# First sweep of a cross-attention: keys projected in quarters and queries in pieces, one a round, each with a PSUM bank of its own

## The chip, the cores and the metric

The kernel runs on one core of one Trainium2 chip. The metric is the device time of one execution in microseconds (us); the figure for the kernel before is the median of three runs.

## The reference

The reference is one block of a Perceiver: a cross-attention of 2 x 512 latent tokens to a context of 2 x 8192 tokens, a windowed self-attention, and a mixture of 16 experts with a shared feed-forward part. The change touches the first part alone:

```python
q = layernorm(x) @ Wq.T + bq          # 2 x 512 tokens, 512 features = 16 heads of 32
k = ctx @ Wk.T + bk                   # 2 x 8192 tokens
v = ctx @ Wv.T + bv
att = einsum('bhqd,bhkd->bhqk', q, k) / sqrt(32)
att = where(mask == 0, -inf, att)
out = einsum('bhqk,bhkd->bhqd', softmax(att, axis=-1), v)
x = x + (out @ Wo.T + bo)
```

All of it is in float32, with the mask and the maxima in bfloat16 inside the kernel where it subtracts them.

## The kernel before, in words

**Units, chunks, slots.** A unit is one batch entry `b` and one group `g` of four heads (128 features): 8 units. The 8192 context tokens of a unit are 16 chunks (`NKC`) of 512 tokens (`KC`). A slot is one chunk of one unit; there are 128 (`NS`). The softmax needs the maximum over all 8192 keys before the first exponential, so the kernel sweeps a unit twice: in slot `n` it projects the keys of chunk `n`, in slot `n + 1` it takes that chunk's maxima (`max_part`), and in slot `n + 18` (`LAG` is 18) it computes the scores again, their exponentials and their products with the values. Three units are thus worked on at a time in most of the kernel. In the first 18 slots, numbered 0 to 17, there is nothing to exponentiate yet: only keys, maxima, the queries, and from slot 16 on the values. The change is about these slots and what comes ahead of them.

**Rounds.** A slot is a loop of four rounds, `i` = 0 to 3 (the `for i in range(4)` of the slot loop). `max_part(slot - 1, i)` handles the query tokens `128 i` to `128 i + 127`. For the first 17 chunks it takes its early form: two double-bank PSUM tiles from the pool `pairs` (3 tiles, 6 banks), each for two heads; four float32 products of 32 x 128 queries by 32 x 512 keys (L276), one for each head, then four one-row bfloat16 products that add the mask row (L282); then VectorE reduces each double tile to its maxima (`tensor_reduce`, L287, 128 x 1024 in, 128 x 2 out, into the SBUF tile `mst`). With three tiles and two used a round, the first tile of a round is free at once, and the second is the one that VectorE reduced first in the round before.

**What else a round holds.** Rounds 0 and 1 of a slot project the two halves of its keys, `project_k(slot, half)`: 16 products with 32-column weights and 256 tokens (L239), four side by side in the four column groups of the array, into one PSUM bank, and one ScalarE instruction that adds the bias and writes SBUF (L243). From slot 16 on, rounds 2 and 3 project the values (L255, then VectorE at L260). Round 3 of slots 1 to 12 takes one entry of the list `later`: three queries of batch 0 (`query(0, g)`), the statistics of batch 1 (`query_norm(1)`), its four transposes (`query_in`, L98), its four queries. A query is four products with 128-column weights and 512 tokens (L173) and a ScalarE instruction (L177). One matmul in the code is two instructions in the trace where its operands are float32.

**PSUM.** During the first 18 slots the pool `ps` has two banks that serve everything but the maxima: transposes, queries, keys, values, and the two small tiles of `max_finish`. At slot 18 these pools close and one of 8 banks opens.

**Order of the work.** Each engine runs its own instructions in order; a scheduler places them nearly as the code writes them. Loads go out on SyncE's queue in the order written, each waiting for its buffer: tokens of batch 0, `wq`, `wk`, context chunk 0, tokens of batch 1, `wv`, then a context chunk (1 MB, 4 buffers) and a mask row for each slot. The mask row of chunk 0 must wait until `mask_rows` has turned the mask and written it to DRAM from ScalarE's queue (L192, L196). Ahead of slot 0 the code normalizes and transposes the four token blocks of batch 0, projects query (0, 0), then calls `mask_rows` and `load_mask(0)`; slot 0 itself projects the keys of chunk 0.

Of the kernel before, what the change touches and what calls it, by code (L numbers as in the profile page):

```python
# [10 lines left out]
F32 = mybir.dt.float32  # L11
# [3 lines left out]
AF = mybir.ActivationFunctionType  # L15
ALU = mybir.AluOpType
AX = mybir.AxisListType
PSUM = bass.MemoryType.PSUM

P = 128  # L20
B, S, D = 2, 512, 512
T = B * S
S2 = 8192
H, DK = 16, 32
G = 4
DC = D // P
# [8 lines left out]
KC = 512  # L35
NKC = S2 // KC
# [7 lines left out]
def perceiver_kernel(  # L44
# [8 lines left out]
    nc = tc.nc  # L53
# [8 lines left out]
    def load_x(b):  # L62
        nc.sync.dma_start(
            out=x_sb[:, ts(b, NT // B), :],
            in_=x[ts(b, S), :].rearrange("(n p) d -> p n d", p=P),
        )
# [22 lines left out]
    def normalized(dst, n, mv, rs):  # L89
        nc.vector.tensor_scalar(  # L90
            dst, x_sb[:, n, :], mv[:, n, 0:1], rs[:, n : n + 1], ALU.subtract, ALU.mult
        )

    def transposed(dst, src, ps):

        tp = ps.tile([P, 4, P], F32, tag="ps", name="tp")
        for c in range(4):
            nc.tensor.transpose(tp[:, c, :], src[:, ts(c, P)], ident)  # L98
        nc.scalar.copy(dst, tp)
# [17 lines left out]
    with ExitStack() as es:  # L117
# [5 lines left out]
        pp = es.enter_context(tc.tile_pool(name="a_p", bufs=4))  # L123
        dram = es.enter_context(tc.tile_pool(name="a_dram", bufs=1, space=bass.MemoryType.DRAM))

        first_ps = ExitStack()
        ps = first_ps.enter_context(tc.tile_pool(name="a_ps1", bufs=2, space=PSUM))
        pairs = first_ps.enter_context(tc.tile_pool(name="a_pairs", bufs=3, space=PSUM))

        def load_w(src, pool, tag):  # L130
            t = pool.tile([P, DC, D], F32, tag=tag, name=tag)
            nc.sync.dma_start(out=t, in_=src.rearrange("(c p) f -> p c f", p=P))
            return t

        bq_c = cp.tile([P, G], F32, name="bq_c")
# [15 lines left out]
        nc.vector.memset(mrep, 0.0)  # L151
        junk = cp.tile([P, KC], BF16, name="junk")

        wq_sb = load_w(wq, pp, "p")
        wk_sb = load_w(wk, cp, "wk_sb")


        qT = cp.tile([P, G, T], F32, name="qT")
        xnT, ln = {}, {}

        def query_norm(b):
            ln[b] = layernorm_stats(tmp, range(b * (NT // B), (b + 1) * (NT // B)))
            xnT[b] = pp.tile([P, DC, S], F32, tag="p", name="xnT")

        def query_in(b, c):
            xn = tmp.tile([P, D], F32, tag="row", name="xn")
            normalized(xn, b * (NT // B) + c, *ln[b])
            transposed(xnT[b][:, :, ts(c, P)], xn, ps)

        def query(b, g):  # L170
            pq = ps.tile([P, S], F32, tag="ps", name="pq")
            for c in range(DC):
                nc.tensor.matmul(  # L173
                    pq, lhsT=wq_sb[:, c, ts(g, P)], rhs=xnT[b][:, c, :],
                    start=(c == 0), stop=(c == DC - 1),
                )
            nc.scalar.activation(qT[:, g, ts(b, S)], pq, AF.Identity, bias=bq_c[:, g : g + 1])  # L177

        mbias = cp.tile([P, B, S2 // P], F32, name="mbias")
        mrow = dram.tile([B, S2 // P, P], F32, name="mrow")  # L180
# [2 lines left out]
        def mask_rows():  # L183


            nc.vector.tensor_scalar(mbias, mask_i, 0.0, -BIG, ALU.is_equal, ALU.mult)
            for b in range(B):
                tp = ps.tile([P, P], F32, tag="ps", name="tpk")
                nc.tensor.transpose(tp[0 : S2 // P, :], mbias[:, b, :], ident)
                mt = tmp.tile([S2 // P, P], F32, name="mt")  # L190
                nc.scalar.copy(mt, tp[0 : S2 // P, :])
                nc.scalar.dma_start(out=mrow[b], in_=mt)  # L192
                if b == 0:
                    mh = tmp.tile([S2 // P, P], BF16, name="mh")
                    nc.scalar.mul(mh, tp[0 : S2 // P, :], -1.0)
                    nc.scalar.dma_start(out=mrow_h, in_=mh)  # L196
# [3 lines left out]
        NS = len(chunks)  # L200
# [3 lines left out]
        def load(slot):  # L204

            for b, j in {(units[u][0], j) for u, j in wanted(slot)}:
                t = ctxp.tile([P, DC, KC], F32, tag="ctx", name="ctx_t")
                nc.sync.dma_start(
                    out=t, in_=ctxT[b, :, ts(j, KC)].rearrange("(c p) s -> p c s", p=P)
                )  # L210
                ctx_t[slot, b] = t

        def load_mask(slot):

            u, j = chunks[slot]
            early = slot + 1 < LAG
            t = mp.tile(
                [P, KC], BF16 if early else F32, tag="mkh" if early else "mk", name="mk", bufs=3
            )
            rows = mrow_h if early else mrow[units[u][0]]  # L220
            nc.sync.dma_start(
                out=t,
                in_=rows[ts(j, KC // P), :].rearrange("c p -> (c p)").partition_broadcast(P),
            )
            mk_t[slot] = t

        def wanted(slot):
            return [chunks[s] for s in (slot, slot - NKC) if 0 <= s < NS]

        def project_k(slot, half):  # L230
            u, j = chunks[slot]
            b, g = units[u]
            if half == 0:
                k_t[slot] = kp.tile([P, KC], F32, tag="k", name="kt")
            hs = ts(half, KC // 2)
            pk = ps.tile([P, KC // 2], F32, tag="ps", name="pk")
            for c in range(DC):
                for h in range(4):
                    nc.tensor.matmul(  # L239
                        pk[ts(h, DK), :], lhsT=wk_sb[:, c, ds(g * P + h * DK, DK)],  # L240
                        rhs=ctx_t[slot, b][:, c, hs], start=(c == 0), stop=(c == DC - 1),
                    )
            nc.scalar.activation(k_t[slot][:, hs], pk, AF.Identity, bias=bk_c[:, g : g + 1])  # L243
# [138 lines left out]


        load(0)
        load_x(1)
        wv_sb = load_w(wv, cp, "wv_sb")
        query_norm(0)
        for c in range(NT // B):
            query_in(0, c)
        query(0, 0)  # L390
        mask_rows()
        load_mask(0)
        later = [lambda g=g: query(0, g) for g in range(1, G)]
        later += [lambda: query_norm(1)]
        later += [lambda c=c: query_in(1, c) for c in range(NT // B)]
        later += [lambda g=g: query(1, g) for g in range(G)]

        waiting = None
        for slot in range(NS + LAG):
            if slot == LAG:  # L400
                first_ps.close()
                ps = es.enter_context(tc.tile_pool(name="a_ps", bufs=8, space=PSUM))
            if slot + 1 < NS + NKC:
                load(slot + 1)
            elif slot + 1 == NS + NKC:
                wo_sb = load_w(wo, ctxp, "ctx")
                wqkv_t = [load_w(wqkv[:, ts(i, D)], ctxp, "ctx") for i in range(3)]
            if slot + 1 < NS:
                load_mask(slot + 1)
            s = slot - LAG  # L410
            for i in range(4):
                if 1 <= slot <= NS:
                    max_part(slot - 1, i)
                if s >= 0:
                    scores(s, i)
                if waiting is not None:
                    values(*waiting)
                waiting = (s, i) if s >= 0 else None
                if s >= NKC and chunks[s][1] == 1:
                    finish(chunks[s][0] - 1, i)  # L420
                if i < 2 and slot < NS:
                    project_k(slot, i)
                if i == 3 and slot > 0 and later:
                    later.pop(0)()
                if i >= 2 and NKC <= slot < NS + NKC:
                    project_v(slot, i - 2)
            if 1 <= slot <= NS and chunks[slot - 1][1] == NKC - 1:
                max_finish(chunks[slot - 1][0])
# [23 lines left out]
    ps = ctx.enter_context(tc.tile_pool(name="c_ps", bufs=8, space=PSUM))  # L452
# [21 lines left out]
    xnT, aT, hT = {}, {}, {}  # L474


    with ExitStack() as es:
# [249 lines left out]
        for k in range(len(items) + 3):  # L727
            i, n = divmod(k, NBQ)
# [74 lines left out]
    for b in range(B):  # L803
        sT = sTp.tile([P, SH // P, S], F32, tag="sT", name="sT")
        for f in range(SH // P):
            pair = []
            for wts in (shg, shu):
                pf = ps.tile([P, S], F32, tag="ps", name="pf")
                for c in range(DC):
                    nc.tensor.matmul(  # L810
                        pf, lhsT=wts[f // 4][:, c, ts(f % 4, P)], rhs=hT[b][:, c, :],
                        start=(c == 0), stop=(c == DC - 1),
# [17 lines left out]
        for j in range(4):  # L830
            po = ps.tile([P, D], F32, tag="ps", name="pso")
            for f in range(SH // P):
                nc.tensor.matmul(  # L833
                    po, lhsT=sT[:, f, ts(j, P)], rhs=shd[f // 4][:, f % 4, :],
                    start=(f == 0), stop=(f == SH // P - 1),
# [120 lines left out]
```

## Time and profile before

| what | value |
|---|---|
| median of 3 runs | 3814.18 us (3814.16 to 3819.29) |
| profiled execution | 3813.35 us |
| its span, first to last instruction | 3811.6 us |
| PE busy in the span | 3741.4 us, 98% |
| VectorE (DVE) busy | 2293.9 us, 60% |
| ScalarE (ACT) busy | 1601.8 us, 42% |
| GpSimd (POOL) busy | 2069.0 us, 54% |
| first reduction of a maximum (L287) | at 28.28 us |
| first product of slot 18 (L295) | at 254.19 us |

The span is 1.75 us shorter than the time of its execution. In the profile PE is the matmul unit and PEld its weight loads. A row of the timeline gives start, duration, engine, line, operation, the program's names as out<-in, shapes and count, and in brackets how long the engine was idle before it and what ended the idling. Matmuls are pipelined: several are in flight at once, so the start of one group to the start of the next is what a group costs, and its printed duration is a little longer.

### The profile page before, as it was taken

The page shows a single profiled execution, that of the slowest core. Times are in us where ns is not written, and L with a number is a line of the kernel's source. Part 1 is how long each engine was busy: PE and PEld are TensorE (multiplying, and loading weights), DVE is VectorE, ACT ScalarE, POOL GpSimd, SP SyncE. Part 2 cuts the span into 40 slices and gives each one's busy share as a digit, 9 for nine tenths or more (in the row PEclk, how much of TensorE's full clock was granted, in tenths as well). Part 3 has the DMA queues.
Part 4 walks back from the last instruction along what each step waited for, and adds up shares of the span by engine and source line. Part 5 has one row for each costly group of instructions (what it writes and reads, how often), then busy time and mean ns, then how long its engine had stood idle before and what let it go on. Part 6 is the DMA issues. An engine that isn't in the chain of part 4 may idle for free.

```text
span 3811.6 us, 99469 instructions
## 1 busy us (share of the span) xinstructions
PE 3741.4 (98%) x43060; PEld 1835.4 (48%) x43060; DVE 2293.9 (60%) x5420; ACT 1601.8 (42%) x2965; POOL 2069.0 (54%) x523
## 2 busy tenths in 40 slices
PE   8999999999999999999999999999999999999998
PEld 3345554554554555555455455444454444444444
DVE  5777777777777777777777777799853600000000
ACT  1125555555555555555555555677463001111110
POOL 0029998998998998899899899600200000000000
PEclk9999999999999999999999999999999999999999
DMA  5222211222213333222222122222201178888885
GB/s 189 89 73 71 71 62 66 71 71 71 69 63 111 122 120 104 61 68 71 71 71 71 57 71 71 71 79 71 80 25 43 61 240 287 288 286 287 287 284 172
DMA packets 143735, 438.07 MB, mean 115 GB/s; under 512 B 9408, under 2 KB 11728, under 8 KB 117856
## 3 DMA queue, kind: packets, MB, share of 16 engines
q1 hardware_dynamic: 137856, 419.33, 33.0%
q0 software_dynamic: 5200, 12.30, 1.3%
q8 instruction: 337, 5.52, 0.6%
q14 instruction: 102, 0.84, 0.1%
q10 hardware_dynamic: 240, 0.08, 0.0%
HBM read 423.21 MB, written 8.47 MB: 113 GB/s over the span
## 4 chain that ended last, share of the span: by engine, by line
PE 87%; DVE 2%; ACT 2%; issue 1%; DMA 0%; POOLq 0%; DVEq 0%; ACTq 0%
PE av L353 13%; PE sx L295 12%; PE sc L331 12%; PE pv L255 11%; PE pf L857 11%; PE pk L239 10%; PE py L875 5%; PE pf L810 3%; PE sc L337 3%; PE po L106 2%; PE pqkv L535 2%; PE pso L833 1%; PE tp L98 1%; DVE junk L300 1%; ACT sb L611 1%
## 5 line engine op out<-in xcount | busy, mean ns | idle before, releaser
L365 POOL TENSOR_TENSOR acc<-acc,pt 128x2048 f32<-128x2048 f32 x437 | 1991.9, 4558 | 445.6 <-ACT pt L344 444.9
L344 ACT ACTIVATE pt<-sc,mbias 128x512 f32<-128x512 f32 x2016 | 1220.1, 690 | 951.2 <-PE sc L337 949.7
L300 DVE CUSTOM_DVE_ANT_0 junk<-sx,mk 128x512 bf16<-128x512 f32 x1776 | 1228.1, 691 | 550.0 <-PE sx L295 352.7
L331 PE MATMUL sc<-qT,kt 32*128 32x512 f32 x4096 | 546.4, 594 | 0.0
L353 PE MATMUL av<-pt,vt 128*32 128x512 f32 x4032 | 540.6, 605 | 2.8 <-DVE mst L300 2.8
L255 PEld LDWEIGHTS pv<-wv_sb,ctx_t 128*32 128x32 f32 x16384 | 457.6, 110 | 155.0 <-DVE mst L300 101.4
L295 PE MATMUL sx<-kt,qT 32*128 32x512 f32 x3552 | 509.1, 640 | 0.9 <-DVE vt L260 0.9
L239 PE MATMUL pk<-ctx_t,wk_sb 128*32 128x256 f32 x8192 | 497.5, 384 | 2.1 <-DVE mst L300 2.1
L255 PE MATMUL pv<-wv_sb,ctx_t 128*32 128x128 f32 x16384 | 495.1, 273 | 1.3 <-DVE avs L361 1.3
L857 PE MATMUL pf<-wt,xinT 128*128 128x512 f32 x1024 | 459.4, 593 | 1.1
L239 PEld LDWEIGHTS pk<-ctx_t,wk_sb 128*32 128x32 f32 x8192 | 263.3, 111 | 295.7 <-DVE mst L300 104.7
L361 DVE TENSOR_TENSOR avs<-av,avs 128x512 f32<-128x512 f32 x504 | 345.4, 685 | 2.7 <-PE av L353 2.5
L331 PEld LDWEIGHTS sc<-qT,kt 32*128 32x128 f32 x4096 | 245.6, 184 | 201.0 <-issue 160.3
L864 DVE TENSOR_TENSOR eo<-pf,sg 128x512 f32<-128x512 f32 x64 | 44.3, 692 | 459.0 <-PE pf L857 459.0
L857 PEld LDWEIGHTS pf<-wt,xinT 128*128 128x128 f32 x1024 | 193.0, 190 | 221.0 <-issue 213.2
L786 POOL DMA_INDIRECT xin<-h_dram,idx x16 | 15.9, 992 | 435.1 <-PE tp L98 310.0
L881 POOL DMA_INDIRECT out_x<-y,idx x16 | 25.3, 1579 | 408.9 <-DVE y L880 408.9
L353 PEld LDWEIGHTS av<-pt,vt 128*32 128x32 f32 x4032 | 81.7, 108 | 325.9 <-DVE mst L300 281.0
L875 PE MATMUL py<-wt,eoT 128*128 128x512 f32 x512 | 222.3, 592 | 0.0
L862 ACT ACTIVATE sg<-pf 128x512 f32<-128x512 f32 x64 | 38.2, 597 | 426.9 <-PE pf L857 426.9
L337 PE MATMUL sc<-mT,neg 32*128 32x512 bf16 x2048 | 207.8, 374 | 0.0
L295 PEld LDWEIGHTS sx<-kt,qT 32*128 32x128 f32 x3552 | 139.9, 182 | 138.2 <-DVE mst L300 92.3
(159 smaller groups left out, 2471.1 us busy)
## 6 DMA issues: line engine op xcount, KB each, us to landing
ctx_t<-in_ctxT SPq DMA_DIRECT2D x160, 1024.0 KB, 6.0
wt<-in_gw SPq DMA_DIRECT2D x64, 1024.0 KB, 4.9
wt<-in_up SPq DMA_DIRECT2D x64, 1024.0 KB, 4.9
wt<-in_down SPq DMA_DIRECT2D x64, 1024.0 KB, 6.3
mk<-mrow SPq DMA_DIRECT2D x111, 256.0 KB, 3.5
ctx<-in_wqkv SPq DMA_DIRECT2D x3, 1024.0 KB, 5.1
mk<-mrow_h SPq DMA_DIRECT2D x17, 128.0 KB, 2.9
x_sb<-in_x SPq DMA_DIRECT2D x2, 1024.0 KB, 10.7
```

The costliest lines, as they stand in the source:

```text
L239: nc.tensor.matmul(pk[ts(h, DK), :], lhsT=wk_sb[:, c, ds(g * P + h * DK, DK)], rhs=ctx_t[slot, b][:, c, hs], start=(c == 0), stop=(c == DC ...
L255: nc.tensor.matmul(pv[ts(k, DK), i, :], lhsT=ctx_t[slot, b][:, c, ds((2 * half + i) * P + k * DK, DK)], rhs=wv_sb[:, c, ts(g, P)], start=( ...
L295: nc.tensor.matmul(sm, lhsT=qT[r, g, ds(b * S + c * P, P)], rhs=k_t[s][r, :], start=True, stop=True)
L300: nc.vector.tensor_tensor_reduce(out=junk, in0=ss[h], in1=mk_t[s], scale=1.0, scalar=-3.0e38, op0=ALU.add, op1=ALU.max, accum_out=mst[u][: ...
L331: nc.tensor.matmul(sc, lhsT=k_t[s][r, ts(ch, P)], rhs=qT[r, g, ts(b, S)], start=True, stop=False)
L337: nc.tensor.matmul(ss[h], lhsT=neg[r, :], rhs=m_t[u][r, :], start=False, stop=True)
L344: nc.scalar.activation(pt[:, h, :], ss[h], AF.Exp, bias=mbias[:, b, cc : cc + 1], scale=SCALE)
L353: nc.tensor.matmul(av[ts(h, DK), :], lhsT=v_t[s][:, ch, ts(h, DK)], rhs=pt_t[s, ch][:, h, :], start=True, stop=True,)
L361: nc.vector.tensor_tensor(avs[u], av, avs[u], ALU.add)
L365: eng.tensor_tensor(acc[u], acc[u], pt_t[s, ch], ALU.add)
L857: nc.tensor.matmul(pf, lhsT=xinT[:, c, :], rhs=wt[:, c, :], start=False, stop=(c == DC - 1))
L875: nc.tensor.matmul(py, lhsT=eoT[:, fq * 4 + c, :], rhs=wt[:, c, :], start=False, stop=(fq == FQ - 1 and c == 3),)
```

## The change

- `project_k` takes a number of parts. In slots 1 to 15 the keys of a slot are projected in quarters of 128 tokens, one a round: quarter 0 of a slot in round 3 of the slot before it, quarters 1 to 3 in its rounds 0 to 2. Slot 0's four quarters stand ahead of the loop. Slots 16 and later keep halves.
- A query is projected in eight pieces: two halves of 256 tokens, each over the four 128-feature chunks of the contraction, one chunk a piece. The weights are taken 32 columns at a time, four side by side as the keys' are. One piece is popped from `later` in each round, from round 0 of slot 0 on, where before one whole entry was popped in round 3. The list has 61 entries in place of 12.
- The two banks of `ps` become `ps` with one bank (keys, values, one mask transpose, `max_finish`) and `ps_q` with one bank (token transposes, queries, the other mask transpose). `pairs` stays as it is.
- Ahead of the loop, `wq` is loaded after `wk` and context chunk 0; `mask_rows` and `load_mask(0)` are called ahead of the normalization; the keys of chunk 0 come ahead of query (0, 0).
- In words the change also says that the maxima stay in PSUM. `max_part` is the same in both kernels.

```diff
-        ps = first_ps.enter_context(tc.tile_pool(name="a_ps1", bufs=2, space=PSUM))
+        ps = first_ps.enter_context(tc.tile_pool(name="a_ps1", bufs=1, space=PSUM))
+        ps_q = first_ps.enter_context(tc.tile_pool(name="a_psq", bufs=1, space=PSUM))
...
-        wq_sb = load_w(wq, pp, "p")
         wk_sb = load_w(wk, cp, "wk_sb")
...
-            transposed(xnT[b][:, :, ts(c, P)], xn, ps)
-
-        def query(b, g):
-            pq = ps.tile([P, S], F32, tag="ps", name="pq")
-            for c in range(DC):
+            transposed(xnT[b][:, :, ts(c, P)], xn, ps_q)
+
+        pq = {}
+
+        def query(b, g, half, c):
+
+            if c == 0:
+                pq[0] = ps_q.tile([P, S // 2], F32, tag="ps", name="pq")
+            for h in range(4):
                 nc.tensor.matmul(
-                    pq, lhsT=wq_sb[:, c, ts(g, P)], rhs=xnT[b][:, c, :],
-                    start=(c == 0), stop=(c == DC - 1),
-                )
-            nc.scalar.activation(qT[:, g, ts(b, S)], pq, AF.Identity, bias=bq_c[:, g : g + 1])
+                    pq[0][ts(h, DK), :], lhsT=wq_sb[:, c, ds(g * P + h * DK, DK)],
+                    rhs=xnT[b][:, c, ts(half, S // 2)], start=(c == 0), stop=(c == DC - 1),
+                )
+            if c == DC - 1:
+                nc.scalar.activation(
+                    qT[:, g, ds(b * S + half * (S // 2), S // 2)], pq[0], AF.Identity,
+                    bias=bq_c[:, g : g + 1],
+                )
...
-                tp = ps.tile([P, P], F32, tag="ps", name="tpk")
+                tp = (ps, ps_q)[b].tile([P, P], F32, tag="ps", name="tpk")
...
-        def project_k(slot, half):
+        def project_k(slot, part, parts=2):
...
-            if half == 0:
+            if part == 0:
                 k_t[slot] = kp.tile([P, KC], F32, tag="k", name="kt")
-            hs = ts(half, KC // 2)
-            pk = ps.tile([P, KC // 2], F32, tag="ps", name="pk")
+            hs = ts(part, KC // parts)
+            pk = ps.tile([P, KC // parts], F32, tag="ps", name="pk")
...
         load(0)
+        wq_sb = load_w(wq, pp, "p")
         load_x(1)
         wv_sb = load_w(wv, cp, "wv_sb")
+        mask_rows()
+        load_mask(0)
         query_norm(0)
         for c in range(NT // B):
             query_in(0, c)
-        query(0, 0)
-        mask_rows()
-        load_mask(0)
-        later = [lambda g=g: query(0, g) for g in range(1, G)]
+        for i in range(4):
+            project_k(0, i, 4)
+        halves = [(half, c) for half in range(2) for c in range(DC)]
+        for half, c in halves:
+            query(0, 0, half, c)
+        later = [lambda g=g, p=p: query(0, g, *p) for g in range(1, G) for p in halves]
         later += [lambda: query_norm(1)]
         later += [lambda c=c: query_in(1, c) for c in range(NT // B)]
-        later += [lambda g=g: query(1, g) for g in range(G)]
+        later += [lambda g=g, p=p: query(1, g, *p) for g in range(G) for p in halves]
...
-                ps = es.enter_context(tc.tile_pool(name="a_ps", bufs=8, space=PSUM))
+                ps = ps_q = es.enter_context(tc.tile_pool(name="a_ps", bufs=8, space=PSUM))
...
-                if i < 2 and slot < NS:
+                if slot < NKC:
+
+                    if i < 3 and slot > 0:
+                        project_k(slot, i + 1, 4)
+                    elif i == 3 and slot + 1 < NKC:
+                        project_k(slot + 1, 0, 4)
+                elif i < 2 and slot < NS:
                     project_k(slot, i)
-                if i == 3 and slot > 0 and later:
+                if later:
                     later.pop(0)()
```

## The prediction

> **What bounds the kernel now.** I read the waits of the first 270 us, then VectorE's timeline there, then PE's for single rounds, then the busy time by stage. The chain of work that ended last is of no use here: it is followed back only to 254 us, where slot 18 begins. First VectorE's timeline over one slot with a query (slot 11):
>
> ```profile
> 158.12 2.36 DVE L287 TENSOR_REDUCE mst<-sx 128x2 f32<-128x1024 f32 x2 [2.74 <-PE sx L282]
> 161.27 2.36 DVE L287 TENSOR_REDUCE mst<-sx 128x2 f32<-128x1024 f32 x2 [0.80 <-PE sx L282]
> 164.42 4.83 DVE L287 TENSOR_REDUCE mst<-sx 128x2 f32<-128x1024 f32 x4 [0.80 <-PE sx L282]
> 171.99 2.36 DVE L287 TENSOR_REDUCE mst<-sx 128x2 f32<-128x1024 f32 x2 [2.74 <-PE sx L282]
> ```
>
> The two reductions of a round start at 158.12, 161.27, 164.42 and, inside the x4, some 2.47 later; the next slot's at 171.99. So the rounds take 3.15, 3.15, 2.47 and 5.10 us, 13.87 in all, and VectorE works 4 x 2.47 = 9.9 of them. In the short rounds it is VectorE that sets the pace (no idle time), in the others PE keeps it waiting. PE's timeline shows what it does in a round of each kind:
>
> ```profile
> 35.84 0.40 PE L282 MATMUL sx<-mk,neg 1*128 1x512 bf16 x4
> 36.06 1.02 PE L276 MATMUL sx<-kt,qT 32*128 32x512 f32 x4
> 37.55 0.70 PE L276 MATMUL sx<-kt,qT 32*128 32x512 f32 x2 [0.46 <-DVE mst L287]
> ...
> 38.82 3.70 PE L173 MATMUL pq<-xnT,p 128*128 128x512 f32 x8
> 42.45 1.14 PE L276 MATMUL sx<-kt,qT 32*128 32x512 f32 x8
> 43.41 0.40 PE L282 MATMUL sx<-mk,neg 1*128 1x512 bf16 x4
> 43.74 0.64 PE L239 MATMUL pk<-ctx_t,wk_sb 128*32 128x256 f32 x8
> ```
>
> The maxima of a round cost PE 43.74 - 42.45 = 1.29 us when nothing holds them, a query 42.45 - 38.82 = 3.63. In rounds 2 and 3 the maxima wait for a bank (the 0.46, released by VectorE). Then the query comes in one lump of 3.63 and VectorE starves. PE and VectorE take turns; neither is full. The busy time by stage (PE, PEld, DVE, ACT, POOL) says it again, against a stretch of the main part below it:
>
> ```profile
> 158.00:172.00 14.00, 13.54 (x128) 5.48 (x128) 9.44 (x9) 1.64 (x3) 0.00 (x0) 1.00 0.27 85
> 206.00:220.00 14.00, 12.96 (x130) 5.02 (x124) 11.37 (x10) 0.95 (x2) 0.00 (x0) 1.00 0.43 124
> 300.00:350.00 50.00, 50.00 (x776) 25.10 (x772) 37.21 (x98) 26.80 (x46) 46.84 (x11) 1.00 0.17 55
> ```
>
> PE's 13.54 of 14 looks full but is time in flight. What the instructions of slot 11 need, 4 x 1.29 + 2 x 1.86 + 3.63, is 12.5 of 13.87. From 254 us on PE waits for nothing.
>
> [...] a half of the keys takes 1.86 us where row-tiled products stand on both sides of it (33.02 to 34.88), and 1.73 in the main part, where the products ahead of it are column-tiled too:
>
> ```profile
> 262.93 1.73 PE pk L239 x32
> 264.65 1.07 PE sx L295 x8
> ...
> 267.79 1.75 PE pv L255 x64
> ```
>
> I put 0.13 on the switching of a round. [...] Here the granted clock is 0.5 for such windows at 82.9, 195.5 (two), 222.8 and 239.9 us, each after two or more rounds with little but maxima on PE; there a half of the keys takes 3.6 in place of 1.9 us.
>
> **The change, part by part.**
>
> *Quarters.* A quarter is 16 products of 128 columns in place of a half's 16 of 256. Does it cost half? The values' row is the nearest: 64 instructions of 128 columns, with 64 weight loads, take 1.75 us beside 1.73 for 32 of 256. So narrow products cost by columns here, and a quarter is 0.87 of streaming plus 0.13 of switching: 1.00. From above, if each instruction had a fixed price, it would be 1.86.
>
> *Query pieces.* 4 products of 32-column weights and 256 tokens, 8 instructions. The keys' half is 32 of the same form in 1.73, so 0.43 a piece and 3.46 a query, as before (3.63). They follow the keys in the same tiling mode, so I add no switch; with one it is 0.56.
>
> *A round with both* costs PE 1.29 + 1.00 + 0.43 = 2.72, VectorE 2.47. PE sets it, and it is steady: the second tile waits for a reduction that ended about when it is asked for, so up to 0.1 may be added, and nothing may be taken off below 2.47. A round with a transpose: 1.29 + 1.00 + 0.58 (93.51 to 94.09) = 2.87; for the two with a normalization (0.54) on VectorE, 3.0. A round with no piece: PE 2.29, so VectorE's 2.47.
>
> *One bank each.* A quarter's bank must be emptied (ScalarE, 0.47 us for 256 columns, less for 128) before the next quarter. About 1.7 us of other PE work lies between, so nothing; if that cover went, some 0.5 a round. Query pieces: the same, with over 2 us between. ScalarE gets 32 key evictions more, and 8 of 256 query columns more, in place of idle time (110.2 us waiting for keys between 60 and 270 us): nothing. From slot 16 on, keys and values share one bank. Values of round 3 wait for VectorE's 0.42 us eviction, which comes behind 2.47 of reductions and ends about when PE gets there: 0 to 0.3 a slot.
>
> *The start.* SyncE's queue: keys and chunk 0 ahead of `wq`. Loads land some 2.7 us apart (1 MB at 380 GB/s), so wk at 10.8, chunk 0 at 13.5, wq at 16.2, wv about 21.6. The mask is turned at 11 us, where PE waits anyway for tokens. ScalarE's three DMA issues (0.45 to 0.54 each) now precede the transposes' evictions, while PE still waits for chunk 0. The mask is in DRAM at about 12.5 + 4.6 = 17, where before it was at 24.7. The first products then no longer wait 2.70 for the mask row. But chunk 1, which was issued at 9.8, now stands behind that mask row on SyncE and lands at 24 to 25. In the changed kernel's order as built PE needs it for slot 1's first quarter, ahead of the first maxima. PE's own work to there, at full clock: transposes 2.3, slot 0's keys 3.7, 12 query pieces 5.2, a quarter 0.9, 12.1 in all; from 13.5 to 18 at half clock that does 2.25, the rest ends at 27.9, and the first reduction is at 29.2 (now 28.28): +0.9. If chunk 1 is late, up to 4 more.
>
> *Nothing else moves.* The maxima stay where they were, and the slots from 18 on are the same instructions.
>
> **The sum.** Before: slots 1 to 15 run from 28.28 to 223.0, 194.7 us; slots 16 and 17 from there to 254.19, 31.2. After, `later` has four pieces in slot 0, so 57 of its 61 entries meet maxima: 52 rounds with query pieces, 52 x 2.72 = 141.4; 4 with transposes, 2 x 2.87 + 2 x 3.0 = 11.7; the round of `query_norm` and the last three of slot 15, 4 x 2.47 = 9.9. Together 163.0: a gain of 31.7. In slot 16 the first round took 4.95 at half clock and should take 3.15[...]: 1.8 more. The start gives back 0.9. In all -32.6. 3813.35 - 32.6 = 3780.7 for an execution like the profiled one, which is 0.83 below the median shown. I predict 3781.
>
> **Rivals.**
> 1. *VectorE's floor.* If key and query products follow each other without the switch, a round is 2.59 or VectorE's 2.47: 52 x 0.2 = 10 less, and slot 17's slow window (1.7) goes too: about 3769. For it: PE reads no slower than that in the main part. Against: the 1.86 beside it.
> 2. *Waits in the round or at the start.* Chunk 1 lands late (+4), or each piece costs a switch (0.13) and a bank wait (0.1) more, 52 x 0.23 = 12: 3785 to 3795, say 3792. For it: three kinds of products in a round. Against: both banks have 1.7 us and more of cover.
> 3. *Slower: fixed price of a matmul.* [...] If the 32 instructions of a quarter cost what 32 of a half do, 1.86, the round is 1.29 + 1.86 + 0.43 = 3.58: 52 x 0.86 = 45 more, and the other eight rounds about 0.8 each, so 3781 + 51 = 3832. It decides from where a round exceeds 2.72 + 32.6/52 = 3.35. Against: the values' 64 instructions in 1.75 us.
> 4. *It doesn't do what it says, or the gain is given back.* Main part and POOL are untouched and PE never waits there, so a head start is kept. Only 0.02 for no change.
>
> **Chances.** Forecast (3774 to 3786) 0.60; VectorE's floor 0.17; extra waits 0.17; fixed price 0.04; no change 0.02. The range reaches to both middle rivals: 3768 to 3793. A measurement of this kernel tells 0.2%, 7.6 us, from no change; so faster 0.94, same 0.02, slower 0.04.
>
> **What would show it.** Right: VectorE's reductions of slots 1 to 15 in pairs 2.7 us apart without the 5.1 steps; a quarter of 1.0 from start to start; no window of 0.5 clock between 35 and 215 us; first reduction near 29; first product of slot 18 at about 221.6. Wrong: pairs over 3 us apart, with PE waiting for ScalarE's evictions or with quarters near 1.9; a stop for chunk 1; or a main part longer than its 3557 us (254 us to the end).

## The result and the profile after

| | before | changed |
|---|---|---|
| median of 4 runs each | 3815.3 us (3814.16 to 3819.29) | 3784.41 us (3783.58 to 3786.64) |
| ratio, 95% interval | | 0.9918 (0.9901 to 0.9935) |
| profiled execution, its span | 3813.35, 3811.6 us | 3783.58, 3781.8 us |
| first reduction of a maximum | 28.28 us | 33.01 us |
| slots 1 to 15, from there | 194.7 us | 163.6 us |
| slots 16 and 17 | 31.2 us | 28.1 us |
| first product of slot 18 | 254.19 us | 224.71 us |
| from there to the end | 3557.4 us | 3557.1 us |

The kernel is faster, by 0.8%. The forecast was 3781 with a range from 3768 to 3793. VectorE's timeline of the changed kernel, over the same stretch as shown of before:

```profile
159.18 2.36 DVE L296 TENSOR_REDUCE mst<-sx 128x2 f32<-128x1024 f32 x2 [0.37 <-PE sx L291]
161.91 2.36 DVE L296 TENSOR_REDUCE mst<-sx 128x2 f32<-128x1024 f32 x2 [0.37 <-PE sx L291]
164.64 2.36 DVE L296 TENSOR_REDUCE mst<-sx 128x2 f32<-128x1024 f32 x2 [0.38 <-PE sx L291]
167.37 2.36 DVE L296 TENSOR_REDUCE mst<-sx 128x2 f32<-128x1024 f32 x2 [0.37 <-PE sx L291]
...
```

The steps of 3.15, 3.15, 2.47 and 5.10 have become one step of 2.73, each with the same short wait for PE: VectorE idles 0.37 us in each round, where it idled 0.80, 0.80, 0.11 and 2.74. (The 0.11 is too short for the view to print: the row of four reductions before takes 4.83, and two pairs of 2.36 are 4.72.) PE's timeline shows what a round now consists of:

```profile
102.63 0.61 PE L178 MATMUL pq<-xnT,p 128*32 128x256 f32 x8
103.17 1.14 PE L285 MATMUL sx<-kt,qT 32*128 32x512 f32 x8
104.14 0.40 PE L291 MATMUL sx<-mk,neg 1*128 1x512 bf16 x4
104.46 1.08 PE L248 MATMUL pk<-ctx_t,wk_sb 128*32 128x128 f32 x32
105.36 0.61 PE L178 MATMUL pq<-xnT,p 128*32 128x256 f32 x8
105.91 1.14 PE L285 MATMUL sx<-kt,qT 32*128 32x512 f32 x8
```

From start to start: maxima 0.97 + 0.32, quarter 0.90, query piece 0.55; none of these rows shows a wait. The busy time of two of the stretches (columns as before: PE, PEld, DVE, ACT, POOL, clock, DMA):

```profile
158.00:172.00 14.00, 14.00 (x267) 7.40 (x266) 12.13 (x11) 2.31 (x6) 0.00 (x0) 1.00 0.28 87
300.00:350.00 50.00, 50.00 (x780) 25.01 (x772) 37.21 (x99) 26.99 (x46) 46.79 (x11) 1.00 0.24 81
```

In the first, VectorE's 9.44 has become 12.13 and PE has no gap. The second, of the main part, is as it was (PE 50.00 of 50.00 in both kernels). What came out otherwise than forecast is the start, on PE's timeline:

```profile
14.70 1.46 PE L248 MATMUL pk<-ctx_t,wk_sb 128*32 128x128 f32 x18 [3.08 <-DMA ctx_t<-in_ctxT]
16.09 1.11 PE L98 MATMUL tp<-ident,xn 128*128 128x128 f32 x4
17.13 1.08 PE L248 MATMUL pk<-ctx_t,wk_sb 128*32 128x128 f32 x14
18.14 1.09 PE L98 MATMUL tp<-ident,xn 128*128 128x128 f32 x4
...
26.80 1.93 PE L178 MATMUL pq<-xnT,p 128*32 128x256 f32 x32 [0.57 <-ACT qT L183]
...
29.32 1.50 PE L178 MATMUL pq<-xnT,p 128*32 128x256 f32 x24 [0.16 <-ACT qT L183]
```

The transposes, whose tokens are there from 10.7 us on, stand behind keys that wait for chunk 0 until 14.70. The queries wait twice until ScalarE has emptied their single bank (0.57 and 0.16). The first products of the maxima come at 31.62; the prediction had them at 27.9. The trace has the clock as full from 19.06 on and no record of it ahead of that, where PE ran at little more than half the pace: four transposes take 1.04 us from start to start at 16.09, and 0.59 at 19.93. Below, this is the rise of the clock.

### The profile page after: what moved, and what is told of

It is laid out like the page before. It is cut to its first block, busy times and chain, and to the rows that moved or that the text cites. A ratio compares the mean times of both kernels' runs of the same rounds, so it can differ in the third digit from the quotient of the medians.

```text
span 3781.8 us, 102452 instructions
## 1 busy us (share of the span) xinstructions
PE 3719.0 (98%) x44532; PEld 1850.7 (49%) x44532; DVE 2294.2 (61%) x5420; ACT 1610.1 (43%) x3005; POOL 2068.3 (55%) x523
## 4 chain that ended last, share of the span: by engine, by line
PE 88%; DVE 2%; ACT 2%; issue 1%; DMA 0%; POOLq 0%; DVEq 0%; ACTq 0%; SPq 0%
PE av L362 13%; PE sx L304 12%; PE sc L340 12%; PE pv L264 11%; PE pf L877 11%; PE pk L248 10%; PE py L895 5%; PE pf L830 3%; PE sc L346 3%; PE po L106 2%; PE pso L853 1%; PE pqkv L555 1%; PE tp L98 1%; DVE junk L309 1%; ACT sb L631 1%
## 5 line engine op out<-in xcount | busy, mean ns | idle before, releaser
L248 PE MATMUL pk<-ctx_t,wk_sb 128*32 128x256 f32 (+1 forms) x9216 | 499.3, 357 | 5.3 <-DMA ctx_t<-in_ctxT 3.1
L248 PEld LDWEIGHTS pk<-ctx_t,wk_sb 128*32 128x32 f32 x9216 | 284.0, 110 | 297.8 <-DVE mst L309 104.7
L252 ACT ACTIVATE kt<-pk,bk_c 128x256 f32<-128x256 f32 (+1 forms) x288 | 129.5, 450 | 219.7 <-PE pk L248 219.7
```

Source lines behind the costliest of these rows:

```text
L248: nc.tensor.matmul(pk[ts(h, DK), :], lhsT=wk_sb[:, c, ds(g * P + h * DK, DK)], rhs=ctx_t[slot, b][:, c, hs], start=(c == 0), stop=(c == DC ...
```

## The experiments

The columns give the median, the first reduction and the first product of slot 18 in the profiled execution, and the usual steps of a slot's rounds at full clock.

| kernel | median us | first reduction | slot 18 | rounds us |
|---|---|---|---|---|
| before | 3815.3 | 28.28 | 254.19 | 3.15, 3.15, 2.47, 2.47 or 5.10 |
| changed | 3784.41 | 33.01 | 224.71 | 2.73 |
| quarters only | 3794.43 | 30.63 | 234.97 | 2.47 x3, 2.47, 3.06 or 6.11 |
| pieces only | 3805.91 | 32.26 | 247.45 | 3.76, 3.58, 2.47, 2.47 |
| no mask products | 3770.79 | 32.74 | 212.54 | 2.51 |
| both banks at the start | 3781.39 | 30.48 | 222.47 | 2.73 |
| old start | 3784.42 | 32.41 | 225.73 | 2.73 |
| before, filled | 3805.58 | 28.18 | 247.84 | as before, but 3.06 last in slots 5 to 8 |
| pieces from slot 1 | 3785.51 | 30.38 | 223.02 | 2.73 |
| changed, again | 3783.93 | 33.02 | 224.73 | 2.73 |
| both banks, pieces from slot 1 | 3781.36 | 29.62 | 223.89 | 2.73 |
| shared banks | 3780.96 | 29.73 | 221.30 | 2.73 |
| products of 64 columns | 3795.67 | 33.56 | 237.68 | 2.75, some 3.8 to 4.6 |

**One part alone: quarters.**

```diff
-        later = [lambda g=g, p=p: query(0, g, *p) for g in range(1, G) for p in halves]
+        later = [lambda g=g: query(0, g) for g in range(1, G)]
...
-                if later:
+                if i == 3 and slot > 0 and later:
```

The body of `query` is again that of before, in the bank `ps_q`, and query (0, 0) and those of batch 1 are whole again too.

> The changed kernel with its queries put back: whole queries of four 128-column products, one in round 3 of slots 1 to 12; keys stay in quarters. Theory (a round costs the longer of PE's work and VectorE's 2.47 us): rounds without a query fall to 2.47, the seven with one cost about 6.0 (1.29 + 1.00 + 3.63), so a slot is 13.4 with a query and 9.9 without; slots 1 to 15 take about 176 us, and the time is about 3795. Rival (the spread queries bring all of the gain, the quarters nothing): near the time before, 3812 to 3815.

3794.43 us, ratio to before 0.9951 (0.9936 to 0.9966). VectorE's timeline over one slot:

```profile
150.14 9.78 DVE L288 TENSOR_REDUCE mst<-sx 128x2 f32<-128x1024 f32 x8 [3.75 <-PE sx L283]
163.68 2.36 DVE L288 TENSOR_REDUCE mst<-sx 128x2 f32<-128x1024 f32 x2 [3.75 <-PE sx L283]
```

Four rounds follow each other in one row, then VectorE starves for 3.75 us while PE does a whole query: 13.54 a slot, 13.4 expected. Slot 18 begins 19.2 us earlier than before. The rival is out.

**One part alone: query pieces.**

```diff
-        for i in range(4):
-            project_k(0, i, 4)
...
-                if slot < NKC:
-
-                    if i < 3 and slot > 0:
-                        project_k(slot, i + 1, 4)
-                    elif i == 3 and slot + 1 < NKC:
-                        project_k(slot + 1, 0, 4)
-                elif i < 2 and slot < NS:
+                if i < 2 and slot < NS:
                     project_k(slot, i)
```

> The changed kernel with its keys put back in halves in rounds 0 and 1 (slot 0's too); queries stay in pieces, one a round. Theory: rounds 0 and 1 cost PE 1.29 + 1.86 + 0.43 = 3.58, rounds 2 and 3 VectorE's 2.47; a slot is 12.1, slots 1 to 15 take about 181 us, and the time is about 3801. Rival (the spread queries bring all of the gain): the time of the changed kernel, 3784.

3805.91 us, ratio 0.9978 (0.9970 to 0.9985). VectorE's timeline:

```profile
122.02 2.36 DVE L296 TENSOR_REDUCE mst<-sx 128x2 f32<-128x1024 f32 x2 [1.41 <-PE sx L291]
125.60 7.30 DVE L296 TENSOR_REDUCE mst<-sx 128x2 f32<-128x1024 f32 x6 [1.23 <-PE sx L291]
134.31 2.36 DVE L296 TENSOR_REDUCE mst<-sx 128x2 f32<-128x1024 f32 x2 [1.40 <-PE sx L291]
```

The second round is 3.58 as expected (122.02 to 125.60). The next three take 8.71: 2.47 twice, and 3.76 for the first of the next slot, 0.18 more than expected. The kernel before has the same step: its first rounds take 3.33 where the round ahead of them is one of 2.47, and 3.15 elsewhere. In both kernels a round of 2.47 ends with a reduction 0.22 us after the last mask product, and a longer one, in nearly all cases, with a reduction 0.40 after it; so a long round after a short one costs 0.18 more. The 5.10 of the kernel before has it too (1.29 + 3.63 = 4.92), and the 6.11 above (1.29 + 1.00 + 3.63 = 5.92). Slot 18 begins 6.7 us earlier than before, although a half-clock window of 6.8 us fell into slots 16 and 17.

For what the parts are worth, slots 1 to 15 are the fair stretch, since what the new start costs stays out of it. There the quarters alone bring 18.5 us, the pieces alone 10.8, both together 31.1. Each of the three contains some 6.4 us of half-clock rounds that the kernel before alone has in this stretch (see the half clock, below); without them it is about 12, 4.5 and 25. A round costs the longer of two times, so that work moved out of a long round is worth most when no other long round is left.

**What sets the round of 2.73.**

```diff
                     nc.tensor.matmul(
                         two[h // 2][:, h % 2, :], lhsT=qT[r, g, ds(b * S + c * P, P)],
-                        rhs=k_t[s][r, :], start=True, stop=False,
+                        rhs=k_t[s][r, :], start=True, stop=True,
                     )
-                for h in range(4):
-                    r = slice(h * DK, h * DK + 1)
-                    nc.tensor.matmul(
-                        two[h // 2][:, h % 2, :], lhsT=neg[r, :], rhs=mk_t[s][r, :],
-                        start=False, stop=True,
-                    )
```

> The changed kernel without the four one-row products that subtract the mask row from the early maxima: it leaves that part of the maxima out. Theory (PE sets the 2.73 us round): PE needs 0.33 less, 2.40, so VectorE takes over at 2.47; 52 rounds gain 0.26, the others some 3 us in all, time about 3767. Rival (waits for banks or the hand-over between PE and VectorE set the round): rounds stay at 2.7, time 3781 to 3784.

3770.79 us, ratio 0.9887 (0.9872 to 0.9903). PE sets the round: it fell to 2.51. That is 0.22 less, not 0.26: from the start of the maxima to that of the quarter it is 1.07 here, where it was 0.97 + 0.32, so the four products cost 0.22 and not the 0.32 up to the next row; what takes the other 0.10 was not shown. The time fell by 13.6 us where 16 to 17 was expected; a half-clock window in slot 17 is part of that. There is more here than was asked. Where a round holds no query piece it came below 2.47, which the prediction took for VectorE's own pace. VectorE's timeline at the end of slot 15, in this kernel:

```profile
174.04 2.36 DVE L290 TENSOR_REDUCE mst<-sx 128x2 f32<-128x1024 f32 x2 [0.15 <-PE sx L285]
176.56 9.14 DVE L290 TENSOR_REDUCE mst<-sx 128x2 f32<-128x1024 f32 x8 [0.15 <-PE sx L285]
```

and in the changed kernel:

```profile
186.49 2.36 DVE L296 TENSOR_REDUCE mst<-sx 128x2 f32<-128x1024 f32 x2 [0.37 <-PE sx L291]
189.22 9.78 DVE L296 TENSOR_REDUCE mst<-sx 128x2 f32<-128x1024 f32 x8 [0.37 <-PE sx L291]
```

Neither prints any idling inside its row, yet eight reductions take 9.14 in one and 9.78 in the other. In the first each reduction starts 1.13 after the one before; in the second the steps are 1.14 inside a round and 1.33 from one round to the next, with 0.11 idle there. VectorE's own pace is thus 2.26 a round, and the 2.47 is a loop through PE. PE's timeline of the changed kernel shows it:

```profile
195.45 0.19 PEld L285 LDWEIGHTS sx<-kt,qT 32*128 32x128 f32 x2 [0.96 <-DVE mst L296]
195.47 0.09 PEld L291 LDWEIGHTS <-neg 1*128 1x128 bf16 x2
...
195.99 0.59 PE L285 MATMUL sx<-kt,qT 32*128 32x512 f32 x2
...
196.42 0.38 PE L291 MATMUL sx<-mk,neg 1*128 1x512 bf16 x2
```

The second tile of a round can be filled only when the first tile of the round before is reduced (at 195.40). Its products follow at 195.45 and 195.99, its mask products at 196.42, and 0.22 later, at 196.65, VectorE starts the next round, whose first tile had its last product by 195.86: 1.23 + 0.05 + 0.54 + 0.43 + 0.22 = 2.47. Without the 0.43 of the mask products this loop would take 2.04, so the 2.26 of the other kernel isn't the loop's. In every round of slots 1 to 17, in each of the twelve kernels that have mask products, the reduction of a first tile starts 0.21 us or more after the last mask product of its round, never before it. So it evidently waits for the products of the second tile too. No run took that wait alone away.

**The half clock.** The kernel before, with products whose result isn't read:

```diff
+                if i >= 2 and slot in (4, 5, 6, 7, 8, 13, 14, 15):
+                    fill = ps.tile([P, P], F32, tag="ps", name="fill")
+                    for c in range(DC):
+                        for h in range(4):
+                            nc.tensor.matmul(
+                                fill[ts(h, DK), :], lhsT=wk_sb[:, c, ts(h, DK)],
+                                rhs=ctx_t[slot, 0][:, c, 0:P],
+                                start=(c == 0), stop=(c == DC - 1),
+                            )
```

> The kernel before, with a quarter's worth of products of no use (about 1.0 us, result not read) in rounds 2 and 3 of slots 4 to 8 and 13 to 15, where PE had little but maxima. Theory (these rounds wait on the hand-over between PE and VectorE, so PE's filling costs nothing, and it keeps the clock up): no half-clock window at 82.9, 195.5 and 222.8 us, the first rounds of slots 5, 14 and 16 fall from 5.0 to 5.4 us to 3.2 to 3.3, and the time falls by about 6 us. Rival (the windows do not come from idling): windows stay, time unchanged or up to 5 us longer.

3805.58 us beside 3813.12 for the kernel before, ratio 0.9978 (0.9969 to 0.9987): more work, and 7.5 us less. In the profile of the kernel before the granted clock is 0.50 for 3.41 us each from 28.24, 82.86, 222.80 and 239.87 us on, and for 6.83 us from 195.50 on. Busy time by stretch, of the kernel before (the clock is the column after POOL):

```profile
80.00:94.00 14.00, 13.42 (x120) 5.10 (x116) 10.26 (x10) 0.95 (x2) 0.00 (x0) 0.88 0.35 113
194.00:204.00 10.00, 10.00 (x74) 3.46 (x74) 5.75 (x6) 0.48 (x1) 0.00 (x0) 0.66 0.19 70
220.00:228.00 8.00, 7.88 (x66) 2.66 (x64) 5.17 (x6) 0.47 (x1) 0.00 (x0) 0.79 0.18 67
```

and of the filled one:

```profile
80.00:94.00 14.00, 14.00 (x212) 6.93 (x212) 11.75 (x11) 1.53 (x3) 0.00 (x0) 1.00 0.39 119
194.00:204.00 10.00, 10.00 (x162) 4.81 (x158) 8.00 (x8) 0.95 (x2) 0.00 (x0) 1.00 0.40 120
220.00:228.00 8.00, 8.00 (x154) 4.41 (x152) 6.24 (x6) 0.95 (x2) 0.00 (x0) 1.00 0.38 127
```

The three windows are gone, and the first rounds of slots 5, 14 and 16 take 3.32 to 3.33 us. One window of 3.4 us came at 179.6 instead, after the maxima of rounds 2 and 3 of slot 12, which were not filled. Slot 18 begins 6.4 us earlier than before. Not all of that is the filling. Two more windows of the kernel before, at 28.2 and 239.9 us, are gone too, although nothing was filled there, so chance has a part in where windows fall; and the filling lengthened the last rounds of slots 5 to 8, which hold a transpose too, by 0.3 to 0.6 us, so it was not free everywhere.

An estimate from the excess of each half-clock round over its like at full clock: in the profile of the kernel before the windows cost 1.7 us in slot 1, 1.6 in slot 5, 3.1 in slots 13 and 14, 1.6 in slot 16 and 1.5 in slot 17, 9.5 in all. In the changed kernel the clock is full from 19.06 us to beyond 2800. So up to 9.5 us of the change's 29.5 are clock, not order; by the medians the filled kernel won 7.5.

**The start.** First its order, put back:

```diff
+        wq_sb = load_w(wq, pp, "p")
         wk_sb = load_w(wk, cp, "wk_sb")
...
-        wq_sb = load_w(wq, pp, "p")
...
-        mask_rows()
-        load_mask(0)
         query_norm(0)
         for c in range(NT // B):
             query_in(0, c)
-        for i in range(4):
-            project_k(0, i, 4)
         for half, c in halves:
             query(0, 0, half, c)
+        mask_rows()
+        load_mask(0)
+        for i in range(4):
+            project_k(0, i, 4)
```

> The changed kernel with the order of the start put back (wq loaded first, query (0, 0) and the mask ahead of the keys of chunk 0); rounds and banks as changed. Theory (the changed start is what came out 3.8 us late, because its transposes stand behind keys that wait for chunk 0): transposes run from 10.5 us on, the first reduction comes at 28 to 29, the rounds stay 2.73, and the time is about 3780. Rival (keys first is the better start, and the loads set it): first reduction at 33 or later, time 3784 to 3788.

3784.42 us, and the first reduction at 32.41: a miss of the theory. Three of four transposes did run from 10.65 us on, but keys that wait for chunk 0 (16.23) still stand ahead of the fourth in the order of the built kernel, and the clock rose only at 21.49. Slot 18 begins 1.0 us later than in the changed kernel; a half-clock window in slot 17 cost this one 1.65. The old order gained nothing in time; with the loads, the mask, the keys and the rise of the clock all different at once, the run doesn't say what each is worth. Second, both banks ahead of slot 0 (`query` and `project_k` take the bank as an argument):

```diff
-            transposed(xnT[b][:, :, ts(c, P)], xn, ps_q)
+            transposed(xnT[b][:, :, ts(c, P)], xn, ps if b == 0 and c % 2 else ps_q)
...
-            project_k(0, i, 4)
+            project_k(0, i, 4, ps if i % 2 else ps_q)
...
-            query(0, 0, half, c)
+            query(0, 0, half, c, ps if half else ps_q)
```

> The changed kernel whose first transposes, first four quarters of keys and first query alternate between both banks ahead of slot 0, so that the transposes stand ahead of the keys on PE. Theory (the late first maximum comes from transposes that wait behind keys for the first context chunk, and from waits for a single bank): first reduction 3 to 4 us earlier, at 29 to 30, time about 3781. Rival (landing of wq or of chunk 1 sets the start): at most 1 us earlier, time 3783 to 3784.

3781.39 us as expected, first reduction at 30.48, which is 2.5 us earlier where 3 to 4 were expected. PE's timeline:

```profile
12.85 1.12 PE L98 MATMUL tp<-ident,xn 128*128 128x128 f32 x4 [0.31 <-ACT mh L204]
14.15 1.11 PE L98 MATMUL tp<-ident,xn 128*128 128x128 f32 x4 [0.18 <-ACT mt L200]
15.99 1.94 PE L98 MATMUL tp<-ident,xn 128*128 128x128 f32 x8 [0.73 <-ACT xnT L99]
17.96 4.87 PE L248 MATMUL pk<-ctx_t,wk_sb 128*32 128x128 f32 x128
22.66 5.20 PE L178 MATMUL pq<-xnT,p 128*32 128x256 f32 x88
```

All transposes come ahead of all keys, and from 17.96 on the rows show no wait of PE, although the clock rose later than in the changed kernel (20.43 against 19.06). At least 2.5 us of the late start are thus the order of transposes and keys and the waits for single banks; the run doesn't part these two. Third, work moved out of the start:

```diff
-                if later:
+                if slot > 0 and later:
```

> The changed kernel with no query piece in slot 0: the list starts in slot 1 and ends four rounds later, in round 0 of slot 16. Theory (PE sets the round, so a piece costs the same wherever it stands): first reduction 1.7 us earlier, the last three rounds of slot 15 2.73 in place of 2.47 and the first of slot 16 longer by 0.4; time within 1 us of the changed kernel, 3783.5. Rival (work taken out of the start is gained): 1.7 us less or more.

3785.51 us from four runs between 3780.77 and 3786.53, which doesn't tell 1.7 us. The profile does: first reduction 2.6 us earlier (some 0.6 of it by the clock, which rose at 17.78 in place of 19.06; an estimate, half of the 1.28 between), then 0.5 more in slot 15 (two rounds of 2.73 in place of 2.47, not three) and 0.4 in slot 16, nearly as the theory has it. Last, both edits at once, beside the changed kernel on the same chip.

> The changed kernel itself once more, beside the next one: rounds of 2.73, first reduction between 31 and 33 us [...], 3784 us.

> The changed kernel with both banks shared ahead of slot 0 and no query piece in slot 0. Theory (PE sets rounds and start; both edits take waits or half-clock work out of the start): first reduction at 28 to 29 us, the last rounds of slots 15 and 16 0.3 to 0.4 longer, time 3780 to 3781, 3 to 4 below the changed kernel beside it. Rival (the start is set by the landings of chunk 0, chunk 1 and the mask row): 0 to 1 below it.

3783.93 and 3781.36 us: 2.6 less, a little under the 3 to 4 expected, and the first reduction came at 29.62, not at 28 to 29. In its profile slot 18 begins only 0.8 us earlier, because a half-clock window fell into slot 17, where its first round took 4.98 in place of 3.34.

**Banks of their own.**

```diff
-        ps = first_ps.enter_context(tc.tile_pool(name="a_ps1", bufs=1, space=PSUM))
-        ps_q = first_ps.enter_context(tc.tile_pool(name="a_psq", bufs=1, space=PSUM))
+        ps = ps_q = first_ps.enter_context(tc.tile_pool(name="a_ps1", bufs=2, space=PSUM))
```

> The changed kernel with its two single banks made one pool of two again, for keys, queries, values and transposes. Theory (in the rounds a bank is always empty again before it is asked for): rounds stay 2.73; ahead of slot 0 two banks for all let the transposes go first, so the first reduction is at 30 to 31 and the time 3781 to 3782. Rival (a query's accumulation holds a bank over four rounds, so that without banks of their own keys and queries wait for each other): rounds of 2.9 to 3.2, time 3790 or more.

3780.96 us, rounds 2.73, first reduction at 29.73. So this part of the change brings nothing in the rounds, and it costs some 2 us at the start: of the 3.3 us by which the first reduction is earlier, about 1.3 are clock, which rose at 16.39 in place of 19.06 (an estimate, half of the 2.67 between). The rival shows once, at the start: PE idles 2.10 us up to 23.87, until ScalarE has emptied a bank of keys that a query needs. This kernel and the two others that use both banks at the start are the fastest that keep the whole computation, 3 us under the changed one: less than one measurement tells, but repeated in three kernels and visible in each trace.

**How narrow a product may be.** The fixed price of the third rival, looked for at 64 columns:

```diff
-            for c in range(DC):
-                for h in range(4):
-                    nc.tensor.matmul(
-                        pk[ts(h, DK), :], lhsT=wk_sb[:, c, ds(g * P + h * DK, DK)],
-                        rhs=ctx_t[slot, b][:, c, hs], start=(c == 0), stop=(c == DC - 1),
-                    )
+            n = KC // 8 if parts == 4 else KC // parts
+            for k in range(KC // parts // n):
+                for c in range(DC):
+                    for h in range(4):
+                        nc.tensor.matmul(
+                            pk[ts(h, DK), ts(k, n)],
+                            lhsT=wk_sb[:, c, ds(g * P + h * DK, DK)],
+                            rhs=ctx_t[slot, b][:, c, ds(part * (KC // parts) + k * n, n)],
+                            start=(c == 0), stop=(c == DC - 1),
+                        )
```

> The changed kernel with each quarter of the keys made of products of 64 columns in place of 128: twice the products and weight loads for the same columns. If products cost by their columns: a quarter stays 0.90 from start to start, rounds 2.73, time 3784. If each costs at least what one of 128 columns does (1.75 us for 64 of the values' products, 27 ns each): a quarter is 1.77, rounds about 3.6, slots 1 to 15 some 50 us longer, time about 3833.

3795.67 us. Neither: most rounds are 2.75, 0.02 more than at 128, so at 64 columns too the price goes by columns. But some are not, and PE's timeline shows one:

```profile
126.42 0.97 PE L250 MATMUL pk<-ctx_t,wk_sb 128*32 128x64 f32 x50
128.94 0.37 PE L250 MATMUL pk<-ctx_t,wk_sb 128*32 128x64 f32 x11 [1.54 <-issue]
```

In the middle of a quarter PE stands 1.54 us with nothing to wait for. Slots 1, 4, 9 and 12 have one such stop each, of 1.0 to 1.8 us from the last start to the next, and an instruction fetch (the DMA queue of kind instruction) starts 0.6 to 1.2 us ahead of each: at 33.3, 69.0, 126.4 and 161.6 us. Slot 2 has a fifth, shorter one: PE's weight loads stand 0.97 us with nothing to wait for up to 49.07, after a fetch at 46.8, and the round takes 3.82. These five fetches start 6.3 to 7.0 us after the fetch before them; of the others between 33 and 203 us only one comes so late (at 104.0), the rest after at most 6.0. The page counts 365 fetches for this kernel and 349 for the changed one, which has no such stop there. Whether PE waited for the fetches was not shown: only the coincidence was seen, no run changed them, and most have no stop behind them. A half-clock window of 6.8 us fell into slots 16 and 17.

## Why the prediction was right

- *The bound.* Right: PE and VectorE took turns. Each part alone and both together give the rounds that the longer of two works gives (2.47, 6.11; 3.58, 2.47; 2.73), but for the 0.18 after a round of 2.47. The short rounds, which I gave to VectorE, belong to the hand-over.
- *Quarters at half price.* Right: 0.90 from start to start in a round, 1.00 forecast with the switch in it. The fixed price is out down to 64 columns of these products, but for the stops.
- *Query pieces.* 0.55 from start to start, against 0.43 and an upper end of 0.56. The 0.13 that I booked with the quarter as a switch seems to stand here, between the piece and the maxima: the quarter is 0.10 cheaper than forecast, the piece 0.12 dearer. The sum of the round, 2.72, was met by 2.73.
- *VectorE's 2.47.* The number held, its name did not: it is the hand-over through the third tile; VectorE alone needs 2.26. The first rival's floor is in truth a floor of this order of products.
- *One bank each, no cost.* Right in the rounds, wrong ahead of slot 0, where quarters follow each other at once and the cover that I named, other PE work, isn't there: some 2 us by the run with shared banks.
- *The start, +0.9.* The term that failed: +4.7. The forecast let PE work through 12.1 us without a gap from the landing of chunk 0 on, at half pace until the clock rises, for which I had put 18. With the keys' start at 14.70 in place of 13.5 that sum grows by 0.6, with the rise at 19.06 in place of 18 by 0.5, and the first maxima would stand at 29.0. They came at 31.62. The other 2.6 I had put at nothing: the order of transposes and keys, and the single banks. The both-banks run took back 2.5 although its clock rose later. The landing of chunk 0 differs by some 2 us and the rise of the clock by 5 among the kernels tried, so this split is good to about 1 us. My worry about chunk 1 was idle.
- *Slots 16 and 17.* I left slot 17 its half-clock window; it was gone too: 28.1 in place of 29.4. That is luck: both profiles of the changed kernel have no window there, but old start, pieces only, products of 64 columns and both banks with pieces from slot 1 have one, with the same keys, values and maxima in slot 17.
- *Sum.* -31.7 forecast and -31.1 measured for slots 1 to 15, +0.9 and +4.7 for the start, -1.8 and -3.1 for slots 16 and 17, 0 and -0.3 for the main part: -32.6 and -29.8 us. The luck of slot 17 hides 1.3 of the 3.8 that the start was off.
- *The clock.* I named the full clock as a gain in slot 16 alone. But the 194.7 us that I set against 163.0 contain the half-clock rounds of slots 1, 5, 13 and 14, some 6.4 us by the estimate above, so the forecast counted on their going without saying so. They went. I also overlooked the window at 28.24 us, which follows the 2.70 us wait for the mask row, and the one at 239.9 doesn't follow rounds of maxima alone: slot 16 projects values there, and PE had waited 1.44 for VectorE.

## What to carry to other kernels

Where two engines hand tiles to each other through few buffers, a round can cost the longer of their works (here PE's 2.73, where VectorE alone needs 2.26): cut side work into pieces that fit the slack of every round rather than put it whole into one, and cut all of it, because the long rounds left keep much of the loss (over slots 1 to 15 the parts alone brought 18.5 and 10.8 us, both together 31.1). Try whether the pieces' products cost by columns (at 64 columns in place of 128 a round here cost 0.02 us more), and look for stops of PE that no wait explains (here five of about 1.0 to 1.8 us). A profile of one execution may hold slow-clock windows that another doesn't (an estimated 9.5 us in the kernel before, none in this stretch of the changed one): price them apart before calling a gain order. At the start, where no other work covered the emptying of a bank, using every bank and keeping work whose data is there ahead of work whose data is still to land brought the first reduction 2.5 us forward.

## What the runs showed of the hardware that I had not expected

- Useless products made a kernel faster: 7.5 us (3805.58 beside 3813.12). In its profile one half-clock window of 3.4 us is left of six between 28 and 244 us.
- A row of reductions in which the view prints no idle time was not at VectorE's pace: 1.24 us from start to start on average (1.14 and 1.33 in turn), with 1.13 possible.
- Twice as many products for the same columns cost 0.02 us in a round, but PE then stopped five times for about 1.0 to 1.8 us with no wait in the profile.
- The kernel before spread over 15 us (3808.43 to 3823.84), the changed one over 4 (3782.37 to 3786.64). The granted clock goes with it: its mean for the kernel before is 0.996 in the executions of 3808 to 3810 us and 0.992 in those of 3821 to 3824, and 0.004 of 3815 us is 15 us. There are 56 executions of the one and 9 of the other, so the two spreads are not quite alike.
